# A graph attention kernel: rows that run on past a group are joined by VectorE in a shared bank instead of by ScalarE and TensorE, and two quads' logits share a bank

## The chip, the cores and the metric

The program runs on one core of one Trainium2 chip. The metric is the time of the whole program on the device in microseconds (us); of several runs the median counts. The other seven cores do nothing.

The engines of the core are TensorE (PE in the profile), VectorE (DVE), ScalarE (ACT), GpSimd (POOL) and SyncE (SP). Each has its own in-order list of instructions. They wait for each other by semaphores: an instruction that has finished adds to its engine's counter, and another engine's instruction starts when that counter has reached a value. I call such an addition a notice.

## The reference

One layer of graph attention over 12500 nodes and 200000 edges. The edges are sorted by destination `tgt`, so the edges of a node are neighbours in the list.

```python
h = relu(layernorm(x))                                  # [12500, 128]
h = (h @ W_node.T).reshape(12500, 4, 32)                # 4 heads of 32
e = (edge_attr @ W_edge.T).reshape(200000, 4, 32)
att = sum(concat([h[src], h[tgt], e], -1) * a, -1)      # [200000, 4]
att = where(att > 0, att, 0.2 * att)
m = maximum(segment_max(att, tgt), 0)
ex = exp(att - m[tgt])
deg = segment_sum(1, tgt)
denom = segment_sum(ex, tgt) + (200000 - deg) * exp(-m)
out = x + segment_sum(ex / denom[tgt] * h[src], tgt)
```

## The kernel before

The edge list is cut into 392 **groups** of 511 edges (four tiles of 128, `J`, with one place left over). Four groups are a **quad** (98 of them, `QG`). The quads are bundled into 28 **supers** of two to four quads, for which the softmax is done at once. A group's edges have at most 96 destinations, its window (`WIN`).

1. A first stage makes a table of node rows in HBM (`table`, 137 numbers a row: four heads of 32 and a one, a count, four source logits) and the target logits (`side`).
2. `fetch(q)` orders a quad's data: edge features and destinations (`fetch_edges`, L297, from SP's queue), a window of `side` and one of `x` for each group (`fetch_windows`, L484), and 16 indirect gathers of table rows by GpSimd (`gather`, L130), one for each 128 edges. The gathered rows live in a ring of eight quads (`ga_all`, L127). A gather into a place of the ring waits until TensorE has read what lay there 32 groups earlier.
3. `logits(q, i)` marks each edge's place in the window (`at`, L523) and adds up on TensorE the target's and the edge's part of the logit (L528, L531) in the bank `lg`. `add_sources` (L534) adds the three pieces up (L543) and the source's part (L545).
4. `softmax(s)` (L563) works in steps on one super: TensorE turns the logits over (`t_ps`), VectorE runs its scans for the running and final maxima, ScalarE takes exponentials, TensorE turns the results back (`ex_ps`, L632, L642). Four of its results go from TensorE to VectorE or ScalarE a step later, two within a step.
5. `sums(q)` (L702) scales a group's rows by its weights (L721), builds the one-hot matrix (`hot`, L725) and multiplies on TensorE: for each group four products into one bank `acc` of 97 rows, 96 for the window and the last one for the destination that may run on into the next group.

What matters here is that last row. A destination can go on in the next group, so the next group's sum must start from the scaled last row of the one before. Before the change this goes round four engines. The group's first edge place is empty: `complete_group` (L663) lets VectorE write the scaled row there (L668), ScalarE copies the count (L672), TensorE does the product with tile 0, which was held back (L673), and ScalarE takes the bank out (`pt`, L674), after which the next group's L668 may start:

```python
nc.vector.tensor_tensor(ga[0:1, i, 0, 0:132], before[96:97, 0:132], fc, op=mult)      # L668
nc.scalar.copy(ga[0:1, i, 0, R_CNT:R_CNT + 1], before[WIN:WIN + 1, R_CNT:R_CNT + 1])  # L672
nc.tensor.matmul(acc, hot[:, i, 0, :], ga[:, i, 0, :], start=False, stop=True)        # L673
nc.scalar.copy(pt[:, i, :], acc)                                                      # L674
```

(The first line is shortened.) `divide` (L735) then makes the quotients and adds `x`, and SP stores each group's window.

The order is written out by hand. `together` takes one step of each list in turn: in a step one group's sums are issued, one group's logits of a later quad, and in a super's first quad one part of the next softmax. The logits run five quads ahead of the sums and the gathers two quads ahead of the logits.

Of the kernel before, what the change touches and what calls it, by code (L numbers as in the profile page):

```python
# [15 lines left out]
P = 128  # L16
# [5 lines left out]
LN2 = 0.6931471805599453  # L22

# [3 lines left out]
J = 4  # L27
# [9 lines left out]
RAW, MORE = 4, 2  # L37
QUADS = 8
SETS = max(NODE_T, QG * J)
PAD = 1 << 20  # L40
# [7 lines left out]
def kernel(  # L48
# [46 lines left out]

    ident = consts.tile([P, P], F32, name="ident")
# [19 lines left out]
    cont = consts.tile([1, G], F32, name="cont")  # L116
    thru = consts.tile([1, G], F32, name="thru")
# [4 lines left out]
    raw = RAW  # L122
    assert raw == 4 < nq and MORE < quads[raw][1]
# [31 lines left out]
    with tc.manual_schedule():  # L155
# [141 lines left out]
        def fetch_edges(q):  # L297
            g0, m = quads[q]
            ea = EA[q] = load.tile([P, QG, 2, P], F32, name="ea")
            nc.sync.dma_start(ea[:, :m], edge_t[:, g0:g0 + m])  # L300
            db = DB[q] = load.tile([WIN, QG, GE], I32, name="db", bufs=2)
            nc.sync.dma_start(db[:, :m, :], dst.rearrange("(g e) -> g e", e=GE)[g0:g0 + m]
                              .unsqueeze(0).to_broadcast([WIN, m, GE]))

        with tc.tile_pool(name="node", bufs=2) as node, tc.tile_pool(
# [10 lines left out]
            def indexed():  # L316
# [27 lines left out]
                yield  # L344


                nc.vector.tensor_scalar(slot[0:1, :, 0], cont, -1.0, None, op0=OP.add)
                nc.vector.tensor_copy(is_last[0:1, :, 0], thru)
# [71 lines left out]
            for b, (t0, T) in enumerate(sets):  # L420
                load_nodes(b + 4)
                if b >= len(sets) - 3 and b - len(sets) + 3 < min(2, nq):
                    fetch_edges(b - len(sets) + 3)
# [36 lines left out]
    with tc.tile_pool(name="work", bufs=2) as work, \  # L460
# [7 lines left out]
        share_ps = const_ps[0:WIN, WIN + G:].rearrange("p (g h) -> p g h", h=H)  # L468
        nc.vector.tensor_copy(lane_ps, lane)
# [9 lines left out]
        def window(g):  # L479
            return nc.values_load(  # L480
                base[0:1, g:g + 1], engines=[mybir.EngineType.SP], min_val=0, max_val=N - 1,
                skip_runtime_bounds_check_because="a destination, which is a node")

        def fetch_windows(q):  # L484
            g0, m = quads[q]
            pw = PW[q] = load.tile([WIN, QG, SIDE], BF16, name="pw")
            xw = XW[q] = work.tile([WIN, QG, D], F32, name="xw", bufs=8)
            at = [window(g0 + i) for i in range(m)]
            for i in range(m):
                nc.sync.dma_start(pw[:, i, :], side[bass.ds(at[i], WIN), :])  # L490
            for i in range(m):
                nc.sync.dma_start(xw[:, i, :], x[bass.ds(at[i], WIN), :])  # L492

        def fetch(q):
            if q not in EA:
                fetch_edges(q)
# [11 lines left out]
        def open_logits(q):  # L508
# [5 lines left out]
            LG[q] = ps.tile([P, QG, J, PIECES, H], F32, name="lg")  # L514
# [41 lines left out]
        def run_on(n):  # L556

            unread = ps.tile([P, QG, J, PIECES, H], F32, name="lg")
            unread = unread.rearrange("p i j k h -> p (i j k h)")[:, 0:P]
            for _ in range(n):  # L560
                nc.tensor.matmul(unread, ident, ones, start=True, stop=True)

        def softmax(s):  # L563
# [15 lines left out]
            low = turned.tile([P, NE], F32, name="low")  # L579
            nc.scalar.mul(low[:R], t_ps[:R, 1:GE], SLOPE)  # L580
            yield
            att = t_ps[:R, 1:GE]
            nc.vector.tensor_tensor(att, att, low[:R], op=OP.max)
# [24 lines left out]
            if s == len(supers) - 1:  # L608
                run_on(8)
# [8 lines left out]
            ex = turned.tile([SBG * H, GE], F32, name="ex")  # L618
            nc.vector.memset(ex[:R, 0:1], 0.0)
            nc.vector.tensor_tensor(ex[:R, 1:GE], low[:R], top, op=OP.subtract)  # L620
            nc.scalar.activation(ex[:R, 1:GE], ex[:R, 1:GE], AF.Exp)  # L621

            fac = turned.tile([SBG * H, 1], F32, name="fac")
            nc.scalar.activation(fac[:R], top[:, 0:1], AF.Exp, bias=col[:R], scale=-1.0)

# [439 lines left out]
```

## Time and profile before

| | |
|---|---|
| median of three runs | 2529.13 us (2528.36 to 2543.53) |
| the profiled execution, its own time | 2525.21 us |
| its span, first to last instruction | 2523.3 us |
| PE busy | 1419.1 us (56%) |
| DVE busy | 1370.4 us (54%) |
| ACT busy | 430.2 us (17%) |
| POOL busy | 1508.5 us (60%) |
| DMA, share of the 16 engines | about 48%, 119 GB/s |
| granted TensorE clock, mean | 0.523 |

The profile is one execution. A row of the groups gives a line, the engine, the operation, the tiles, the count; then busy time, the mean time of one in ns; then the idle time of the engine before these instructions and what ended most of it. A row of the waits says which instruction waited, after the arrow who released it, and then the sum in us, the number and the longest. "Remote" stands where the profile finds no instruction beside the release. "Issue" is idle time in which it finds no wait. The share of busy time is a mean over stages: a preparation until about 300 us, a long even stage until the last gather at about 2405 us, and a tail.

### The profile page before, as it was taken

The numbers are of one execution on the slowest core, as the hardware profiler recorded it, in microseconds if no ns is written. First come the engines' busy times: TensorE is split into PE (matmuls) and PEld (weight loads), VectorE is DVE, ScalarE is ACT, GpSimd is POOL, SyncE is SP. The second block draws the span as 40 slices with busy tenths as digits, with TensorE's granted clock in tenths as the row PEclk, the third lists the DMA queues.
The fourth block names the chain that finished last, engine by engine and source line by source line (L and its number), as shares of the span: only waits on it lengthen the run. The fifth ranks groups of instructions, "written<-read, shape, count | busy, mean of one in ns | idle before, by whom it ended". The sixth has DMA issues, their size and how long they took to land. (4 is left out here: it accounts for less than half of the span.)

```text
span 2523.3 us, 29558 instructions
## 1 busy us (share of the span) xinstructions
PE 1419.1 (56%) x7317; PEld 1267.0 (50%) x7317; DVE 1370.4 (54%) x3333; ACT 430.2 (17%) x1825; POOL 1508.5 (60%) x1609
## 2 busy tenths in 40 slices
PE   4454565555655655655655555555655555546485
PEld 3444554545554544554554545554544554445375
DVE  4543465555555555555555555555555555446486
ACT  3543211111111111111111111111111111111122
POOL 6444556666666666666666666666666666666603
PEclk7665655555555555555555555555555555555556
DMA  5433465455445455445445455455445455444330
GB/s 188 145 100 97 99 148 127 115 125 128 121 122 133 114 132 129 114 122 126 120 119 129 110 123 122 116 131 127 119 119 127 112 130 128 106 104 122 86 91 17
DMA packets 214495, 299.08 MB, mean 119 GB/s; under 512 B 86121, under 2 KB 162153, under 8 KB 204914
## 3 DMA queue, kind: packets, MB, share of 16 engines
q1 hardware_dynamic: 162512, 184.97, 27.7%
q0 software_dynamic: 50112, 109.61, 19.8%
q10 hardware_dynamic: 1698, 2.58, 0.3%
q8 instruction: 61, 1.00, 0.2%
q14 instruction: 112, 0.92, 0.1%
HBM read 270.45 MB, written 26.52 MB: 118 GB/s over the span
## 5 line engine op out<-in xcount | busy, mean ns | idle before, releaser
L139 POOL DMA_INDIRECT ga<-table,srci x1494 | 1419.3, 950 | 868.4 <-issue 402.5
L730 PE MATMUL acc<-ga,hot 128*97 128x137 f32 x2352 | 648.0, 447 | 326.1 <-ACT ga L714 174.3
L730 PEld LDWEIGHTS acc<-ga,hot 128*97 128x97 f32 x2352 | 516.6, 278 | 350.6 <-ACT ga L714 180.1
L668 DVE TENSOR_TENSOR ga<-acc,facs 1x132 f32<-1x132 f32 x391 | 115.9, 297 | 627.0 <-ACT pt L674 501.5
L673 PE MATMUL acc<-ga,hot 128*97 128x137 f32 x784 | 266.9, 443 | 272.0 <-ACT ga L672 150.7
L531 PE MATMUL lg<-wblk,ea 128*128 128x8 f32 x1568 | 410.0, 359 | 0.0
L531 PEld LDWEIGHTS lg<-wblk,ea 128*128 128x128 f32 x1568 | 382.6, 310 | 0.0
L528 PEld LDWEIGHTS <-at 96*128 96x128 bf16 x1568 | 218.2, 167 | 288.6 <-DVE at L523 144.4
L674 ACT COPY pt<-acc 97x137 f32<-97x137 f32 x392 | 107.1, 273 | 1414.1 <-remote 892.0
L673 PEld LDWEIGHTS acc<-ga,hot 128*97 128x97 f32 x784 | 190.4, 279 | 303.2 <-ACT ga L672 170.6
L528 PE MATMUL lg<-pw,at 96*128 96x12 bf16 x1568 | 170.8, 182 | 227.1 <-DVE at L523 125.5
L721 DVE TENSOR_TENSOR ga<-ga,ex_ps 128x528 f32<-128x528 f32 x392 | 269.9, 689 | 35.4 <-remote 35.0
L523 DVE TENSOR_TENSOR at<-const_ps,db 96x512 bf16<-96x512 f32 x392 | 267.1, 683 | 9.4 <-DMA db<-in_dst_dram 3.6
L725 DVE TENSOR_TENSOR hot<-const_ps,slot 128x384 f32<-128x384 f32 x384 | 209.2, 545 | 0.0
L543 DVE TENSOR_REDUCE st<-lg 128x64 f32<-128x192 f32 x98 | 35.0, 357 | 153.7 <-remote 86.9
L672 ACT COPY ga<-acc 1x1 f32<-1x1 f32 x391 | 59.9, 153 | 231.5 <-DVE ga L668 109.3
L139 POOL DMA_INDIRECT ga<-in_x_dram,srci x72 | 68.5, 952 | 39.1 <-issue 21.3
L392 PE MATMUL row_ps<-wcat,hT 128*128 128x137 f32 x198 | 43.7, 377 | 56.0 <-DVE tgt L398 18.9
L632 PE MATMUL ex_ps<-ident,ex 64*128 64x64 f32 (+2 forms) x112 | 18.4, 313 | 96.3 <-ACT ex L621 70.8
L752 DVE TENSOR_TENSOR res<-pt,const_ps 96x512 f32<-96x512 f32 (+2 forms) x102 | 67.5, 662 | 4.4 <-DVE const_ps L748 0.6
L756 DVE TENSOR_TENSOR res<-res,xw 96x512 f32<-96x512 f32 (+1 forms) x99 | 66.8, 675 | 3.4
L392 PEld LDWEIGHTS row_ps<-wcat,hT 128*128 128x128 f32 x198 | 37.5, 269 | 62.0 <-ACT hn L227 16.8
(135 smaller groups left out, 1066.5 us busy)
## 6 DMA issues: line engine op xcount, KB each, us to landing
db<-in_dst_dram SPq DMA_DIRECT2D x98, 768.0 KB
ea<-in_edge_t_dram SPq DMA_DIRECT2D x98, 512.0 KB
ga<-table,srci POOLq DMA_INDIRECT x1494
xw<-in_x_dram SPq DMA_DIRECT2D x392, 48.0 KB
out_dram<-res SPq DMA_DIRECT2D x392, 48.0 KB
pw<-side SPq DMA_DIRECT2D x392, 2.2 KB
table<-row SPq DMA_DIRECT2D x9, 616.5 KB
xt<-in_x_dram SPq DMA_DIRECT2D x9, 576.0 KB
```

The costliest lines, as they stand in the source:

```text
L139: nc.gpsimd.indirect_dma_start(out=ga[:, i, j, 0:width], out_offset=None, in_=rows, in_offset=bass.IndirectOffsetOnAxis(ap=srci[:, g0 + i, ...
L392: nc.tensor.matmul(row_ps[:, t, :ROW], hT[:, t, :], wcat, start=True, stop=True)
L523: nc.vector.tensor_tensor(at[:, i, :], node_ps[0:WIN, g0 + i:g0 + i + 1].to_broadcast([WIN, GE]), db[:, i, :], op=OP.is_equal)
L528: nc.tensor.matmul(lg[:, i, j].rearrange("p k h -> p (k h)"), at[:, i, j * P:(j + 1) * P], sw, start=i + j == 0, stop=False, skip_group_ch ...
L531: nc.tensor.matmul(lg[:, i, 2 * w:2 * w + 2, 0, :], ea[:, i, w, :], wblk, start=False, stop=True, skip_group_check=True)
L668: nc.vector.tensor_tensor(ga[0:1, i, 0, 0:H * HW].rearrange("p (h w) -> p h w", w=HW), before[WIN:WIN + 1, 0:H * HW].rearrange("p (h w) -> ...
L673: nc.tensor.matmul(acc, hot[:, i, 0, :], ga[:, i, 0, :], start=False, stop=True)
L674: nc.scalar.copy(pt[:, i, :], acc)
L721: nc.vector.tensor_tensor(val, val, heads(ex)[:, :, :, g - s0].unsqueeze(3).to_broadcast([P, J, H, HW]), op=OP.mult)
L725: nc.vector.tensor_tensor(hot[:, i, :, 0:WIN], lane_ps.unsqueeze(1).to_broadcast([P, J, WIN]), slot[:, g, :].unsqueeze(2).to_broadcast([P, ...
L730: nc.tensor.matmul(acc, hot[:, i, j, :], ga[:, i, j, :], start=j == 1, stop=False)
L752: nc.vector.tensor_tensor(res[:, :n, :].rearrange("p g (h d) -> p g h d", d=HD), val[:, :, :, 0:HD], share_ps[:, :n, :].unsqueeze(3).to_br ...
```

## The change

- **Own sums.** All four products of a group are issued together, into one of three places (160 columns apart) of a bank that three consecutive groups share (`sums_place`). Nothing is put into the empty edge place. When three groups are in, `close_bank` puts on a list what is to be done from three steps on: one `carry` for each group in successive steps (VectorE multiplies the row before into `carried`, and adds it, times `thru`, to the group's last row in PSUM), and with the third `evict` (VectorE adds the three carried rows to row 0 and the counts `came` to the count column; ScalarE copies the bank to `pt`, in two parts where a quad ends within it). `divide` follows two steps after the quad's last eviction.
- The counts are worked out once in the first stage (`came`), with four small products and a scan.
- The last six quads (`ENDING`) keep the old way; before them `catch_up` empties the list.
- **Shared logits bank.** `lg` becomes one bank with two halves, one for even and one for odd quads. `add_sources` for a quad is called after the next quad's second group has been issued, instead of before its first.
- In `softmax`, the leaky slope (`low`) and the factors' copy go from ScalarE to VectorE; the factor comes out of the exponential of column 0; the exponential of minus the maximum is taken for the whole tile, so that `divide` needs no exponential; the maxima are read by the sums in PSUM instead of from a copy (`xs`). `run_on`, 18 product records in the last super whose result nobody reads, goes.
- A quad's maxima are copied into the gathered rows by one instruction instead of four, and this and the copy of `is_last` are ScalarE's in the first 14 and last 6 quads (`HELPED`) and VectorE's in between.
- `both` is a table in HBM of `x` beside `side`, made in twelve steps by SP while the first quads are fetched. From quad 14 (`APART`) a group's window is one transfer from it instead of two. From then on edge features and destinations are ordered by ScalarE's queue, after the logits two quads earlier. The four window addresses of a quad are loaded together.

The core of the diff:

```diff
+LATER = 3
+ACCS, ACC_AT = 3, 160
+HELPED = 14, 6
+ENDING = 6
+APART = 14
...
+        lg_all = ps.tile([P, 2, QG, J, PIECES, H], F32, name="lg")
...
-            LG[q] = ps.tile([P, QG, J, PIECES, H], F32, name="lg")
+            LG[q] = lg_all[:, q % 2]
...
+        def close_bank():
+            tile, used = state["bank"]
+            state["bank"] = None
+            bank = tile[0:WIN + 1, 0:ACCS * ACC_AT].rearrange("p (k r) -> p k r", r=ACC_AT)
+            bank = bank[:, 0:len(used), 0:ROW]
+            carried = work.tile([WIN + 1, ACCS, H * HW], F32, name="carried")
+            at = state["step"] + LATER
+            for k in range(len(used)):
+                todo.append((at + k, lambda k=k: carry(bank, used, carried, k)))
+            todo.append((at + len(used) - 1, lambda: evict(bank, used, carried)))
+
+        def carry(bank, used, carried, k):
...
+                nc.vector.tensor_tensor(
+                    to.rearrange("p (h w) -> p h w", w=HW),
+                    state["before"][WIN:WIN + 1, 0:H * HW].rearrange("p (h w) -> p h w", w=HW),
+                    fc[:, :, g - s0].unsqueeze(2).to_broadcast([1, H, HW]), op=OP.mult)
+                nc.vector.scalar_tensor_tensor(row, to, thru_l[:, g:g + 1], row,
+                                               op0=OP.mult, op1=OP.add)
...
+            state["before"] = bank[:, k, :]
+
+        def evict(bank, used, carried):
...
+            nc.vector.tensor_tensor(to, to, carried[WIN:WIN + 1, 0:n, :], op=OP.add)
+            nc.vector.tensor_tensor(bank[0:1, :, R_CNT], bank[0:1, :, R_CNT], came[:, g:g + n],
+                                    op=OP.add)
...
+                nc.scalar.copy(PT[q][:, i:i + len(ks), :], bank[:, ks[0]:ks[-1] + 1, :])
...
-            for i in range(m):
-                nc.scalar.copy(ga[:, i, :, R_SRC:R_SRC + H], heads(xs)[:, :, :, g0 - s0 + i])
+            copier(q)(
+                ga[:, :m, :, R_SRC:R_SRC + H],
+                heads(tops_at)[:, :, :, g0 - s0:g0 - s0 + m].rearrange("p j h g -> p g j h"))
...
-                for j in range(1, J):
-                    nc.tensor.matmul(acc, hot[:, i, j, :], ga[:, i, j, :], start=j == 1, stop=False)
-                complete()
-                begun.append((q, i, ga, hot, pt, acc, fc[:, :, g - s0]))
+                if own:
+                    acc = sums_place(q, i)
+                    for j in range(J):
+                        nc.tensor.matmul(acc, hot[:, i, j, :], ga[:, i, j, :], start=j == 0,
+                                         stop=j == J - 1, skip_group_check=True)
+                    if len(state["bank"][1]) == ACCS:
+                        close_bank()
+                    step()
...
         def all_logits(q):
-            flush()
             open_logits(q)
             for i in range(QG):
                 logits(q, i)
                 yield
+                if i == 1:
+                    flush()
+
+            if APART <= q + 2 < nq:
+                fetch_edges(q + 2, nc.scalar)
             state["logits"] = q
```

## The prediction

> **What bounds the kernel now.** The page comes first. No engine is busy for more than 60% of the span, so I look at idle time and what ends it. These are the two rows with the most idle time, and one link of the chain between the groups:
>
> ```profile
> L139 POOL DMA_INDIRECT ga<-table,srci x1494 | 1419.3, 950 | 868.4 <-issue 402.5
> ...
> L668 DVE TENSOR_TENSOR ga<-acc,facs 1x132 f32<-1x132 f32 x391 | 115.9, 297 | 627.0 <-ACT pt L674 501.5
> ...
> L674 ACT COPY pt<-acc 97x137 f32<-97x137 f32 x392 | 107.1, 273 | 1414.1 <-remote 892.0
> ```
>
> VectorE stands still for 627 us before its row copy, mostly for ScalarE's eviction, and the eviction waits for something "remote". Next the waits of GpSimd:
>
> ```profile
> POOL ga L139 <- issue: 423.8, 1384, 1.2
> POOL ga L139 <- remote: 236.6, 103, 3.5
> POOL ga L139 <- PE acc L673: 141.7, 45, 11.0
> ...
> POOL ga L139 <- PE acc L730: 19.4, 12, 2.7
> ```
>
> The 1384 waits of 0.3 us are the plain distance of two gathers, so a gather costs 0.95 + 0.30 = 1.25 us and a quad's sixteen cost 20 us. The last three rows are 160 waits of 2.49 us, **398 us** together, for TensorE's notice that a place of the ring is free. GpSimd does nothing else in the even stage: 20 us and some 4 us of waits are the quad's 24 us. So GpSimd sets the pace, and these 398 us are what can be won there. Why it waits is seen in the timeline (start, duration, instruction, idle before it):
>
> ```profile
> 1250.09 0.95 POOL L139 DMA_INDIRECT ga<-table,srci  x1 [2.58 <-remote]
> ...
> 1251.51 0.27 ACT L674 COPY pt<-acc 97x137 f32<-97x137 f32 x1 [0.86 <-PE acc L673]
> ...
> 1257.25 0.27 ACT L674 COPY pt<-acc 97x137 f32<-97x137 f32 x1 [2.18 <-PE acc L673]
> ...
> 1259.01 0.66 PE L673 MATMUL acc<-ga,hot 128*97 128x137 f32 x2
> ...
> 1264.00 0.95 POOL L139 DMA_INDIRECT ga<-table,srci  x1 [0.30 <-issue]
> ...
> 1267.29 0.27 ACT L674 COPY pt<-acc 97x137 f32<-97x137 f32 x1 [9.26 <-remote]
> ...
> 1267.53 0.94 POOL L139 DMA_INDIRECT ga<-table,srci  x1 [2.58 <-remote]
> ```
>
> The product L673 ends at 1259.67, and its eviction starts 7.6 us later, 2.3 us after GpSimd's last gather ended (1264.95) and together with GpSimd's own next start. Setting each of the 392 evictions against its product in this view, 240 follow within 0.3 us and 136 come over 1 us late. From 400 to 2200 us, of the 136 products that ended within 4.5 us of the start of a run of gathers 3 were late, of the 143 that ended 4.5 to 10.5 us after it 109. After the last gather (2405 us) none of 29 is. **So while gathers run back to back, TensorE's notices stop after about 4.5 us, and come again only about 2.3 us after GpSimd pauses.** GpSimd pauses only when it lacks such a notice itself. Then everything moves on. What of the chip causes this the trace does not show. A cycle is therefore: GpSimd fills as many groups as TensorE finished since the last pause, 5 us each, then waits 2.49 us. With 1494/4 = 373.5 groups and 160 waits TensorE gets only **2.33 groups** further in a cycle. The chain L674, L668, L672, L673 needs a new notice from TensorE for every group: two pass in the open 4.5 us, one more product is done blind, and it stands.
>
> **The change part by part** (against the profiled execution, 2525.2 us, of which 2523.3 span).
>
> *Carry by VectorE.* TensorE no longer waits for an eviction. In the changed order of instructions the carry of a bank waits for TensorE once in three groups, and then for products two steps old. This is the gain; its size is how far TensorE gets in a cycle. In the open 4.5 us one step is noticed (a step without softmax is 3.6 us of VectorE, below). From there TensorE goes on blind until VectorE needs a missing notice: a bank's comes 1 to 3 groups later with two steps of slack, a quad's logits sum 1 to 4 steps later with almost none. The earlier of the two is about 2.5 steps. In a super's softmax quad four results have one step of slack and two have none, so there it is about 2.5 in all, as now. Three quads of 3.7 and one of 2.5 make 16/(12/3.7 + 4/2.5) = 3.3 groups; I take **3.4**, since a few notices trickle through. Then 373.5/3.4 = 110 waits of 2.49 us = 274 us: **-124 us**. The ends: 2.33 stays (0), or no wait is left (-398).
>
> *What VectorE gets.* Added rows 367 times 1x132: nearest L668, 297 ns: 109 us. Eviction's 1x396 addition, 123 times: L325's 1x391 took 550 ns, L756's 96x512 675; 0.6 gives 74, and 18 for the counts at 0.15. `low`: 28 x 0.68 (L583) = 19. Copies of maxima and flags in 78 quads: 0.27 (L545) and 0.2: 36. Factors and column 0: 28 x 0.35 = 10. Sum **266 us**, 1370 to 1636. Bounds are 200 and 330. It lies beside GpSimd's 20 us a quad: VectorE then has 14.3 us a quad (7.7 for the marks and scalings L523, L721, L725, 3.3 for carries and eviction, 2.2 to divide, 0.6 for sums of logits, 0.5 for copies), and in one quad of about four 9 us of softmax (L571 to L629) as well, 23 together. Only the latter exceeds 20; of its roughly 0.9 us of new softmax work I charge half, 28 x 0.45: **+12**. Without that cover all 266 would show.
>
> Here a rule speaks against the change. The Trainium skill, *Perfetto Trace Analysis*, section "Identifying the Most-Contended Engine", takes VectorE's and GpSimd's occupancy as the bound and the busiest engine as the one to relieve. By it VectorE, at 65% the highest, is loaded further: up to +266. By the row, VectorE sits idle for 627 us before L668 alone, and GpSimd's 60% hides another 424 us of issue distance. I follow the rows: 0 outside the softmax.
>
> *Shared logits bank.* By addresses the sum L543 would come two steps after its logits, and its idle time (153.7 us of VectorE) would go. The skill's *PSUM — Partial Sum Buffer*, section "PSUM bank collisions raise a hardware error", demands that engines be kept apart by bank, not by address. The changed order does so: all 98 sums wait for the newest logits in the bank, also those of the other quad. By the addresses I would subtract up to 154 us; by the rule 0, and the wait stays. I take 0. No run here shows a collision.
>
> *ScalarE* loses L672, L714, L681 and the copies for the factors and maxima, and evicts in larger pieces: 430 us fall to some 300, off the path. It gains the edge transfers of 84 quads; one that waits for TensorE (two or more steps back) or for VectorE's newest `at` holds up eviction and exponentials behind it. Their slack is a step; 0, at worst 28 x 1 us.
>
> *SP* issues 8 transfers a quad instead of 14; nobody waits for it now (L523 for `db`: 3.6 us in all): 0. The twelve steps for `both` move some 13 MB among 299; the 24-byte pieces go while two quads lie ready: 0, at worst +10. *TensorE* has the same 3136 products for sums; 18 of `run_on` (2.8 us) go: 0, either way 3. *GpSimd* has the same gathers; four waits a group instead of one cost nothing as long as they are fulfilled, as 0.30 us stays the distance where a wait precedes. *First stage*: +3. *catch_up*: carries and eviction without sums beside, about 5 us twice, half hidden: +5; the tail has no gathers and its rows stay.
>
> Sum: 2525.2 - 124 + 12 + 5 = 2418; the added 3 lies in stages with slack. The median of the runs lies 3.9 above the profiled time: **about 2420 us**.
>
> **The rivals.**
> - *The notices hardly matter any more.* For: outside the softmax nothing but banks and logits asks TensorE, and slack in the ring is eight quads. Against: GpSimd would then never pause, and the notices come only after pauses. With 6.8 groups to a wait, 55 waits: -261, so 2280; the floor with 0 waits is 2150.
> - *Nothing is won.* The logits sum each quad and the two softmax results without slack stop VectorE, which does everything else, just as soon: 2.33 groups remain, 2525 + 17 + 4 = 2546. Also the case in which the delay of the logits sum is one in name only.
> - *Slower: VectorE becomes the bound in the softmax quads.* Now a late notice for the factors or maxima stops ScalarE; then it stops VectorE and all its marks and scalings. If TensorE gets no further per cycle and the new work of these quads (2.7 + 0.9 us) falls after the stop, 28 x 3.6 = 101: 2630. It decides as soon as VectorE's 23 us and its stops (2.3 us each) exceed the 24 us and GpSimd has no free places left. For it: 23 is close. Against: the next quads have 14 us, and the ring evens it out.
>
> **How the numbers follow.** Forecast 0.50, first rival 0.20, nothing won 0.16, slower 0.14. About 1% is what a measurement of this kernel tells from no change. Faster by more than 1% (below 2504): nearly all of the first two and a little of the third, 0.72; within 1%: 0.13; slower 0.15. The forecast's own range is 2350 to 2500. The range for 8 in 10 goes from 2230, which leaves out the ring's floor, to 2545, which takes in most of "nothing won" and leaves out the slow case.
>
> **What would show it.** Right: GpSimd's waits for TensorE number about 110 with still 2.3 to 2.6 us each; the row of idle time before L668 is gone from its successor; VectorE near 1640 us busy; gathers still 1.25 us apart; gather end near 2300 us, then the same tail of some 120 us. The logits sum should be the largest wait of VectorE. Wrong: as many waits as now, or VectorE idle for `facs` and maxima (second and third rival), or waits under 60 (first). If GpSimd's distance grows above 1.25 us, the base of the sum fails.

## The result, and the profile after

The changed kernel takes **2605.93 us** (median of four runs, 2593.63 to 2614.88); the kernel before took 2531.16 us beside it. The ratio is 1.031, 95% interval 1.0265 to 1.0353: **slower by 3%**, where 2420 us and a gain of 4% were forecast. The profiled execution took 2614.88 us, its span is 2613.1 us: 89.8 us more than the span before.

The groups of the changed kernel's profile that answer to the rows shown of before (busy time, mean ns of one, then idle time before and what ended most of it):

```profile
L155 POOL DMA_INDIRECT ga<-table,srci x1494 | 1416.6, 948 | 930.1 <-issue 338.5
...
L597 DVE TENSOR_REDUCE st<-lg 128x64 f32<-128x192 f32 x98 | 35.0, 357 | 474.6 <-remote 432.1
...
L749 ACT COPY pt<-acc 97x137 f32<-97x137 f32 (+1 forms) x184 | 65.4, 389 | 1510.3 <-DVE acc L742 546.5
L731 DVE SCALAR_TENSOR_TENSOR acc<-carried,thru,acc 1x132 f32<-1x132 f32 x367 | 138.9, 379 | 83.5 <-PE acc L845 36.5
L727 DVE TENSOR_TENSOR carried<-acc,facs 1x132 f32<-1x132 f32 x367 | 110.2, 300 | 12.6 <-ACT pt L749 1.3
```

The 627 us of idle time before the carried row are gone: L727 waits 12.6 us. But the sum of a quad's logits, L597, now waits 474.6 us, 432.1 of it for a late notice ("remote"). Its row before the change was

```profile
L543 DVE TENSOR_REDUCE st<-lg 128x64 f32<-128x192 f32 x98 | 35.0, 357 | 153.7 <-remote 86.9 <-issue 31.4 <-PE acc L673 29.1
```

GpSimd's waits now (sum, number, longest):

```profile
POOL ga L155 <- issue: 358.6, 1148, 1.9
POOL ga L155 <- PE acc L845: 324.4, 204, 14.4
POOL ga L155 <- remote: 154.5, 106, 3.6
...
POOL ga L155 <- PE lg L585: 45.3, 67, 2.5
```

Before, the waits for TensorE were 160 with 398 us. Now the last three of these rows are 377 waits with 524 us: more of them, and more time. One stretch of the timeline shows what they look like (start, duration, instruction, idle time before it):

```profile
1105.84 0.94 POOL L155 DMA_INDIRECT ga<-table,srci  x1 [0.30 <-issue]
1105.88 2.14 PE L845 MATMUL acc<-ga,hot 128*97 128x137 f32 x8
...
1110.30 0.52 PE L845 MATMUL acc<-ga,hot 128*97 128x137 f32 x1 [0.35 <-issue]
1110.83 0.94 POOL L155 DMA_INDIRECT ga<-table,srci  x1 [0.30 <-issue]
1111.70 0.39 PE L845 MATMUL acc<-ga,hot 128*97 128x137 f32 x1 [0.88 <-issue]
1112.08 0.94 POOL L155 DMA_INDIRECT ga<-table,srci  x1 [0.30 <-issue]
1113.11 0.61 PE L845 MATMUL acc<-ga,hot 128*97 128x137 f32 x2 [1.02 <-issue]
1113.38 0.94 POOL L155 DMA_INDIRECT ga<-table,srci  x1 [0.36 <-PE acc L845]
...
1117.74 0.36 DVE L597 TENSOR_REDUCE st<-lg 128x64 f32<-128x192 f32 x1 [6.19 <-remote]
1117.75 0.94 POOL L155 DMA_INDIRECT ga<-table,srci  x1 [2.00 <-remote]
```

A group's four products (eight records) took 2.14 us at 1105.88. The next group's eight records come singly or in twos, from 1108.85 to 1115.17, about one or two to each gather, with idle time between them that nothing in the profile explains. VectorE stands at L597 for 6.19 us and starts together with GpSimd's next gather, as ScalarE's eviction did before the change. So TensorE itself stalls in mid-group now; before the change no matmul of the sums or logits from 1050 to 2250 us stood for over 0.25 us behind one of its own line; now 63 records do.

**Where the 89.8 us arise.** I set the first scaling of each quad (L721 before, L835 after) of the two profiles side by side. At quad 12 the changed kernel is 16.8 us behind, at quad 18 19.3, at quad 36 53.6, at quad 90 73.9, at the end 89.8. The loss has four places: 17 us in the first quads, 34 between quads 18 and 36, 20 over the long even stage, 16 from quad 90 on. Of these 16, 14 lie between the middle of quad 91 and the start of quad 92, where `catch_up` empties the list.

**Pauses.** I also took each gather's idle time beyond the plain 0.30 us, after 330 us, and called it a pause from 1.5 us up:

| kernel | pauses | their sum, us | mean | short ones | sum |
|---|---|---|---|---|---|
| before | 133 | 302 | 2.27 | 17 | 17 |
| after | 109 | 316 | 2.90 | 95 | 73 |
| c1_check_apart | 110 | 274 | 2.49 | 99 | 73 |
| c4_sum_first | 111 | 268 | 2.42 | 84 | 60 |
| c3_both | 103 | 251 | 2.44 | 91 | 69 |
| d2_all_three | 117 | 320 | 2.73 | 20 | 16 |
| e1_no_carry | 113 | 268 | 2.37 | 23 | 17 |
| k1_before_pairs | 121 | 262 | 2.17 | 30 | 34 |

Together 319 us before and 389 after. That is 70 us, and the last gather starts 61 us later (2457 instead of 2396, which the text ahead gave as about 2405). The rows of c1 and c4, two runs explained below, add up to 347 and 328 us: the edit of c1 takes 42 of the 70 us away, and that of c4 another 19.

### The profile page after: what moved, and what is told of

The parts are those of the page before. It is cut to its first block, busy times and chain, and to the rows that moved or that the text cites. A ratio compares the mean times of both kernels' runs of the same rounds, so it can differ in the third digit from the quotient of the medians.

```text
span 2613.1 us, 27591 instructions
## 1 busy us (share of the span) xinstructions
PE 1436.7 (55%) x7303; PEld 1259.7 (48%) x7303; DVE 1653.2 (63%) x4169; ACT 240.9 (9%) x638; POOL 1505.5 (58%) x1609
## 5 line engine op out<-in xcount | busy, mean ns | idle before, releaser
L845 PE MATMUL acc<-ga,hot 128*97 128x137 f32 x2944 | 790.7, 444 | 218.7 <-DVE hot L839 111.6
L845 PEld LDWEIGHTS acc<-ga,hot 128*97 128x97 f32 x2944 | 651.4, 278 | 257.9 <-issue 170.9
L582 PEld LDWEIGHTS <-at 96*128 96x128 bf16 x1568 | 202.7, 161 | 539.2 <-DVE at L577 252.6
L582 PE MATMUL lg<-xw,at 96*128 96x12 bf16 x1568 | 171.2, 180 | 442.5 <-DVE at L577 224.0
L597 DVE TENSOR_REDUCE st<-lg 128x64 f32<-128x192 f32 x98 | 35.0, 357 | 474.6 <-remote 432.1
L835 DVE TENSOR_TENSOR ga<-ga,ex_ps 128x528 f32<-128x528 f32 x392 | 270.1, 689 | 34.4 <-ACT ga L826 28.1
L749 ACT COPY pt<-acc 97x137 f32<-97x137 f32 (+1 forms) x184 | 65.4, 389 | 1510.3 <-DVE acc L742 546.5
L731 DVE SCALAR_TENSOR_TENSOR acc<-carried,thru,acc 1x132 f32<-1x132 f32 x367 | 138.9, 379 | 83.5 <-PE acc L845 36.5
L727 DVE TENSOR_TENSOR carried<-acc,facs 1x132 f32<-1x132 f32 x367 | 110.2, 300 | 12.6 <-ACT pt L749 1.3
L625 PE MATMUL t_ps<-ident,U 128*64 128x128 f32 (+2 forms) x112 | 29.5, 418 | 148.9 <-DVE U L599 129.3
L807 POOL TENSOR_SCALAR hot<-lane,slot 128x96 f32<-128x96 f32 x32 | 17.0, 549 | 98.5 <-issue 92.8
L741 DVE TENSOR_TENSOR acc<-acc,carried 1x396 f32<-1x396 f32 x124 | 69.7, 562 | 4.3
```

The costliest lines, as they stand in the source:

```text
L582: nc.tensor.matmul(lg[:, i, j].rearrange("p k h -> p (k h)"), at[:, i, j * P:(j + 1) * P], sw, start=i + j == 0, stop=False, skip_group_ch ...
L727: nc.vector.tensor_tensor(to.rearrange("p (h w) -> p h w", w=HW), state["before"][WIN:WIN + 1, 0:H * HW].rearrange("p (h w) -> p h w", w=H ...
L731: nc.vector.scalar_tensor_tensor(row, to, thru_l[:, g:g + 1], row, op0=OP.mult, op1=OP.add)
L741: nc.vector.tensor_tensor(to, to, carried[WIN:WIN + 1, 0:n, :], op=OP.add)
L835: nc.vector.tensor_tensor(val, val, heads(ex)[:, :, :, g - s0].unsqueeze(3).to_broadcast([P, J, H, HW]), op=OP.mult)
L845: nc.tensor.matmul(acc, hot[:, i, j, :], ga[:, i, j, :], start=j == 0, stop=j == J - 1, skip_group_check=True)
```

## The experiments

Ratios are to the kernel before, in runs on the same chip. The kernel before took 2521 to 2531 us on these chips, except with d1, d2, n0 and n1, where it took 2550; a ratio of that group is not compared with another's to within 1%. Where I give a lag, it is that of a profiled execution behind the profile of before, read as above.

### Two orders inside the change: c1 to c4

The guard `checked()` compares 128 rows of destinations four times. Before the change a step of other work lay between the transfer and the comparison; the change had moved them into one step, on SP's queue. The diff shown with the change leaves this part out. c1 puts a quad between them (one of the four steps that it adds to the guard is shown):

```diff
                 nc.sync.dma_start(rows[:n], dst_rows[g0:g0 + n, 0:NE + 1])
+                yield
                 falls = turned.tile([P, NE], F32, name="low")
```

> The changed kernel with one edit in checked(): between the order of the 128 rows of destinations and their comparison (L931, L933) VectorE gets a whole quad of other work, so that it does not stand at L933 for the transfer. Theory A (the four waits of 54.0 us in all hold up everything, since between quads 24 and 36 the changed kernel falls behind by some 45 us): the wait of L933 is gone, the lag at quad 36 is below 15 us, about 2560 us. Rival B (VectorE has slack there, the ring of gathers covers the stops): within 10 us of 2606.

VectorE's waits from 700 to 980 us in the changed kernel:

```profile
DVE low L933 <- DMA ex<-in_dst_rows_dram: 54.0, 4, 14.1
DVE st L597 <- remote: 31.5, 4, 9.6
```

These four waits are all of the guard's in the kernel. In c1 they are gone, and the lag at quad 36 is 22.6 us instead of 53.6. Measured: **2587.63 us, 1.0265** (1.0226 to 1.0304). Theory A holds for the place, at less than its price: 31 us at quad 36 in the profile, 11 to 21 us in the ratios (after to c1, where the intervals still overlap, and c2 to c3, where they do not).

c2 gives the sum of logits two steps of slack, from quad 8 on (the first eight quads keep their order in a branch that is not shown):

```diff
-            for i in range(QG):
-                logits(q, i)
-                yield
-                if i == 1:
-                    flush()
+            for i in range(0, QG, 2):
+                logits(q, i)
+                logits(q, i + 1)
+                yield
...
+            yield
+            add_sources(q)
+            yield
```

> The changed kernel with the logits of a quad issued two groups a step in its first two steps, and their sum (L597) in the fourth, from quad 8 on: the newest logits in the shared bank are then two steps old for every sum. Theory A (VectorE's wait of 432 us at L597 for TensorE's late notice took the place of the wait at L668 and hides the gain of the carry): the wait at L597 falls below 200 us and the time by 40 to 120 us, to 2490 to 2565. Rival B (GpSimd's own waits set the pace, wherever VectorE stands): L597's wait moves to other VectorE rows, and the time stays within 15 us of 2606.

Measured: **2574.79 us, 1.0213** (1.0186 to 1.0240). VectorE's waits in c2:

```profile
DVE low L629 <- remote: 168.5, 18, 20.0
DVE st L597 <- PE acc L845: 104.9, 42, 8.5
DVE st L597 <- remote: 91.1, 12, 10.8
DVE acc L731 <- remote: 67.4, 12, 12.5
```

L597's idle time falls to 203 us (196 in these two rows), where theory A asked for less than 200; but the softmax's first step (L629) and the carry (L731) now stand for late notices themselves. About 25 us (a ratio lower by 0.0096) are won, below theory A's range. Both theories hold in part: the wait moves, and a little is won.

c3 has both edits.

> Both edits, of c1 and c2. If both theories A hold: 45 us less than c2, 2445 to 2520, faster than the kernel before. If only the first holds: about 2560. If neither: about 2606.

Measured: **2555.02 us, 1.0129** (1.0103 to 1.0154): the two gains roughly add up, but the result stays above the 2520 that was expected at most, and slower than before.

c4 is c1 with `flush()` again ahead of the next quad's first group:

```diff
+            flush()
             open_logits(q)
...
-                if i == 1:
-                    flush()
```

> c1, and in addition the sum of a quad's logits put back ahead of the next quad's first group (as before the change), with the bank still shared. In the changed kernel 28 of the 98 sums come within the softmax's first step and wait for logits issued in the same step (192 us of 477 us), the others one step later. Theory A (the missing slack of these 28 costs): L597's idle time falls by 100 us or more and the time is 15 to 40 us below c1. Rival B (the notice comes only when GpSimd pauses, and a step more or less does not matter): within 10 us of c1.

Measured: **2560.64 us, 1.0155** (1.0126 to 1.0183), 0.011 or some 28 us below c1, as in theory A. By moving the sum behind the second group, the change had put 28 of the 98 sums into the softmax's first step. There the newest logits in the shared bank had been issued in the same step: 192.5 us of idle time before these 28, 6.9 us each, against some 48 us before the change. But c4 moves all 98 sums. From c1 to c4 L597's idle time falls from 477 to 382 us, just short of the 100 us that theory A asked for: 40 of these 96 us at the 28 sums, 55 at the other 70. So the 28 us are not the price of the 28 sums alone. In c4 the lag is 18.4 us at quad 24 and still 19.8 at quad 90: with the guard and the sum put right the even stage is level with the kernel before from there on, and the 31.5 us by which c4's profile is longer arise before quad 24 and after quad 90.

### The order of the products: d1 and d2

```diff
-                    for j in range(J):
+                    for j in reversed(range(J)):
```

This is d1, made on the changed kernel; d2 is the same on c3.

> The changed kernel with the four products of a group issued from tile 3 to tile 0 instead of 0 to 3. A gather into tile 0 then waits for the last product, and the next three need no wait for TensorE (one wait a group as before the change, 360 in all instead of 1438). Theory A (the finer waits hurt: GpSimd goes on gather by gather behind TensorE, with 64 short waits of 0.79 us from 1050 to 2250 us where before there were 9): the short waits go, and 20 to 60 us with them, 2540 to 2585. Rival B (the pace is set by how far TensorE and VectorE get between two pauses, and the same idle time of GpSimd comes in longer pieces): within 12 us of 2606.

> c3_both with the reversed order of products of d1 in addition. If theory A of d1 holds: 20 to 60 us below c3's 2555, so about 2515, level with the kernel before or faster. If B holds: within 12 us of 2555.

d1: **2606.92 us, 1.0226** (1.0197 to 1.0255). d2: **2562.49 us, 1.0048** (1.0034 to 1.0061). The short waits go as expected: from 1050 to 2250 us, 14 in d1 instead of 64. But the pauses grow: all idle time of GpSimd beyond 0.30 us is 360 us in d1 (389 in the changed kernel) and 335 in d2 (320 in c3). By the ratios 20 us are won in both, by absolute medians nothing, as the kernel before was slower on that chip; which of the two is right is not known. The finer waits are not settled as a cost; the idle time mostly goes into longer pieces, as rival B has it.

### Without the gathers, and with gathers that never wait: n0, n1, g1

```diff
-            for j in range(n):
-                nc.gpsimd.indirect_dma_start(
-                    out=ga[:, i, j, 0:width], out_offset=None, in_=rows,
-                    in_offset=bass.IndirectOffsetOnAxis(ap=srci[:, g0 + i, j:j + 1], axis=0))
+            nc.sync.dma_start(ga[:, i, 0:n, 0:width],
+                              rows[0:n * P, 0:width].rearrange("(j p) r -> p j r", p=P))
```

n0 is made on the kernel before, n1 on the changed one. Both leave the choice of rows out, so their outputs are not the layer's; only their times count.

> The kernel before, with each group's four indirect gathers of GpSimd replaced by one plain transfer of 512 fixed rows of the table from SP's queue (same bytes, other rows, so the sources are not the reference's). Theory A (while GpSimd gathers back to back, TensorE's notices come late, and this sets the pace): evictions follow their products within 0.5 us in the even stage, VectorE's idle time before L668 falls below 150 us, time 1900 to 2200. Rival C (something other delays the notices, TensorE itself or ScalarE): the late evictions stay, and the time is within 5% of 2529.

> The changed kernel with the same replacement. Theory A: VectorE's wait at L597 falls from 477 to below 60 us, and VectorE, with 1650 us of work, is then over 85% busy in the even stage and sets the pace: 1850 to 2100, and not faster than n0 by much, as it has 280 us more of VectorE's work. Rival C: L597 keeps its wait, over 2450.

n0: **1967.72 us**; n1: **1994.47 us**. Theory A holds in both. In n0 all 392 evictions follow their product within 0.04 us, and the carry's row waits 123.6 us instead of 627.0. In n1 the largest waits of VectorE are

```profile
DVE low L931 <- DMA ex<-in_dst_rows_dram: 66.7, 4, 21.3
DVE st L595 <- PE lg L583: 38.2, 31, 4.6
```

(lines two lower than in the changed kernel): the sum of logits waits 38.2 us instead of some 475, and the guard's four waits head the list. VectorE is busy for 182.0 of 200 us from 1050 to 1250 us, where n0's is for 139.0. So with the same bytes but without GpSimd's gathers both kernels lose over 550 us. The changed one is then bound by VectorE: from quad 36 to 88 it is 91% busy. There n1 is not slower but faster, 17.2 us a quad against n0's 18.3; the 27 us are lost in the first eight quads, between quads 20 and 26, where the guard is, and at quad 92. Nor do the two price the carry. n0 has a limit of its own, as SP's queue now carries the rows too: VectorE waits 316.3 us there for earlier stores of results.

```profile
DVE res L750 <- DMA out_dram<-res: 316.3, 62, 8.1
```

g1 lets the gathers run without any wait for TensorE:

```diff
-        ga = GA[q] = ga_all[:, q % QUADS]
+        ga = ga_all[:, q % 4]
+        GA[q] = ga if q < 5 else ga_all[:, 4 + q % 4]
```

> The changed kernel with gathers that never wait for TensorE from quad 5 on: they write into four places of the ring that nobody reads, and the sums read four other places that hold zeros (so the output leaves the gathered rows out). Same gathers, same products. Theory A (TensorE's notices come only while GpSimd pauses): the gathers run 1.25 us apart to their end near 2150 us, and sums advance slowly until then and fast after it, or steadily with notices 7 to 10 us late. Rival D (1.48 us a gather): the distance of two gathers grows to about 1.48 us though nothing waits for TensorE, and they end near 2400 us.

Measured: **3803.06 us, 1.51**. Two stretches (busy us of PE, PEld, DVE, ACT, POOL, each with its number of instructions, then clock, DMA share, GB/s), and VectorE's largest wait:

```profile
500.00:2300.00 1800.00, 149.02 (x642) 119.05 (x641) 144.93 (x333) 12.56 (x38) 1382.74 (x1289) 0.50 0.23 59
2300.00:3700.00 1400.00, 1014.21 (x5207) 902.89 (x5208) 1227.44 (x2969) 90.24 (x220) 0.00 (x0) 0.51 0.35 95
```

```profile
DVE st L600 <- remote: 1068.7, 14, 147.8
```

For 1800 us, while gathers come without a pause, VectorE works for 145 us and about two groups are summed in 100 us; once the gathers have ended, it is 22 groups in 100 us. DMA engines are 23% busy, so their bandwidth as a whole is not what is short. And TensorE's own instructions come singly, one to every one or two gathers:

```profile
1402.44 0.17 PE L585 MATMUL lg<-xw,at 96*128 96x12 bf16 x1 [3.12 <-issue]
1403.43 1.10 POOL L158 DMA_INDIRECT ga<-table,srci  x1 [0.30 <-issue]
1403.84 0.10 PEld L585 LDWEIGHTS <-at 96*128 96x128 bf16 x1 [2.70 <-issue]
1404.83 1.10 POOL L158 DMA_INDIRECT ga<-table,srci  x1 [0.30 <-issue]
1405.23 0.17 PE L585 MATMUL lg<-xw,at 96*128 96x12 bf16 x1 [2.62 <-issue]
```

Theory A holds for the sums: slow until the gathers end, fast after it. Rival D is right in one thing: after some 170 gathers without a pause their distance grows from 1.25 to 1.40 us, and the last one starts at 2289 us, between the two theories' ends. So a quad's sixteen gathers cost 22.4 us when nothing ever stops them. If that distance is the floor, the even stage of the kernel before, at 23.8, had only some 1.4 us a quad to give; that is an estimate, for why the distance grows, and whether it would with a few short pauses, no run here shows.

### One release a quad: f0, f1, f2

```diff
-    ga_all = consts.tile([P, QUADS, QG, J, ROW], F32, name="ga")
+    ga_pool = ctx.enter_context(tc.tile_pool(name="ga_pool", bufs=QUADS))
```

f1 is made on c4, f2 on c3, f0 on the kernel before.

> c4 (comparison a quad later, sum first), and the ring of gathered rows made of eight tiles, one for each quad, instead of one block: the first gather of a quad then waits for TensorE to have finished the whole quad eight before, and no other gather waits for it; so only products that somebody else waits for give a notice (1528 notices of TensorE in the program instead of 2286 or more, 90 waits of GpSimd for TensorE instead of 1438). Theory A (TensorE's notices queue up while GpSimd gathers, and stop it and VectorE; fewer notices and fewer stops of GpSimd are faster): at most 100 pauses of some 2.5 us, GpSimd's waits for TensorE below 300 us, 2400 to 2510. Rival D (a gather needs 1.48 us of some shared path, of which 0.23 us show only as pauses; no order of the consumers changes that): a quad keeps its 23.8 us, within 12 us of c4's 1.0155 of before.

> The same ring on c3 (sums of logits two steps late) instead of c4: 1641 notices. Theory A: as f1, within 15 us of it. Rival D: within 12 us of c3's 1.0129 of before.

> The kernel before with the ring of eight tiles alone (2271 notices instead of 2383; 90 waits instead of 359). There every group's carry needs a new notice of TensorE. Theory A: GpSimd pauses at most once a quad, but the chain gets only some 2.6 groups further between two pauses, so the pauses become longer: within 40 us of 2529, either way. Rival D: within 12 us.

f1: **2561.56 us, 1.0145** (1.009 to 1.020). f2: **2670.21 us, 1.059** (1.0528 to 1.0652). f0: **2842.99 us, 1.127** (1.1206 to 1.1333). GpSimd's waits in f0:

```profile
POOL ga L146 <- PE acc L680: 689.4, 83, 32.1
```

Fewer pauses do not help: there are 85 in f1 and f2 and 88 in f0, but their means are 3.94, 5.22 and 7.14 us. A pause lasts until TensorE has got through the whole quad. Theory A's price is wrong in all three. Rival D's time came true in f1 alone; f0's quad takes 27.3 us, not 23.8. Nor do fewer notices end the stalls in mid-group: f1's trace has 1507 notices of TensorE where c4's has 2324, but 118 such stalls from 1050 to 2250 us where c4 has 60. These stalls do not order the kernels either: c3 has 203 and e1 64, and both are faster than the changed kernel with its 63. The Trainium skill, *TensorE: Matmul & The Clock Gate*, section "The cost: per-tile semaphore tail", fits 26.3 ns to each semaphore increment at the end of small matmuls packed into one array; carried over to these products, 817 notices fewer would be an estimate of 21 us. c4 and f1 are equal within their intervals, but f1's pauses changed too, so no run here shows that gain or refutes it. Why f2 is so much worse than f1 stays open.

### What is left: the carry, the tail and the first quads

```diff
-ENDING = 6
+ENDING = 84
```

e1 is d2 with the old carry from quad 14 on.

> d2 with the old carry (VectorE writes the row, product of tile 0 last, eviction by ScalarE) from quad 14 on instead of only in the last six. Theory A (the carry by VectorE buys longer runs between two pauses, but in the even stage GpSimd's gathers leave only some 1.4 us a quad to win, and the tail pays for VectorE's added work): the even stage keeps 23.7 to 24.0 us a quad, the tail after the last gather is 10 to 25 us shorter, 0.990 to 1.000 of before. Rival E (the carry by VectorE does speed up the even stage of d2, and other parts of the change eat it): the even stage slows to over 24.5 us a quad, ratio above 1.015.

Measured: **2496.85 us, 0.9899** (0.9853 to 0.9945), the lowest median of all, below d2's by 66 us, or by 0.015 (some 38 us) in the ratios. From 1050 to 2250 us a quad takes 23.2 us instead of d2's 23.9, and GpSimd's waits in that stretch are

```profile
POOL ga L155 <- issue: 235.8, 742, 1.1
POOL ga L155 <- remote: 99.2, 40, 4.2
POOL ga L155 <- PE lg L585: 37.8, 15, 3.8
POOL ga L155 <- PE acc L788: 26.7, 14, 3.0
```

The tail after the last gather is 131.5 us against d2's 149.7. Theory A holds in sign and in the tail, and the even stage is better than it said: here the carry by VectorE does not merely win nothing, it loses. How much is less sure. h3 and i1 (below) differ in little but the carry too, on chips where the kernel before took 2527.7 and 2527.6 us; there it costs 8.5 us (2524.16 against 2515.66). With it, d2's VectorE has 15.8 us of work a quad, without it 13.3; the pauses are as many (117 and 113) but 2.73 us long instead of 2.37.

h1 keeps the old carry for ten quads at the end, and gives the leaky slope back to ScalarE:

```diff
-HELPED = 14, 6
-ENDING = 6
+HELPED = 14, 10
+ENDING = 10
...
-            nc.vector.tensor_scalar(low[:R], att, SLOPE, None, op0=OP.mult)
+            nc.scalar.mul(low[:R], att, SLOPE)
```

> d2 with the old carry for the last ten quads instead of six, so that the list is emptied while gathers still run, ScalarE's copies for these ten, and the leaky slope on ScalarE as before. Theory A (the tail is bound by VectorE: 119.6 us busy of 156 against 97.0 of 127 before): the stretch after the last gather falls from 150 to about 130 us and the ratio from 1.0048 to 0.994 to 1.000. Rival F (the tail is bound by the chain of TensorE and ScalarE): 1.002 or more.

h2 leaves the joined table out and orders all edges from SP:

```diff
-            if q < APART and q not in EA:
+            if q not in EA:
                 fetch_edges(q, nc.sync)
-            next(join_steps, None)
...
-            if APART <= q + 2 < nq:
-                fetch_edges(q + 2, nc.scalar)
```

> d2 without the joined table and with all edge transfers from SP's queue, as before the change. Theory A (the first 12 quads fall behind by some 13 us while the joined table is made, as its DMA share is 0.89 there from 300 to 400 us against 0.58; nobody waits for SP later): the lag at quad 12 falls below 6 us, ratio 0.998 to 1.002. Rival G (the joined windows and ScalarE's edge transfers help the even stage): no gain or a loss, 1.005 to 1.02.

h3 is both.

> d2 with the edits of h1 and h2 together. If both theories A hold: 0.988 to 0.996 of before, faster than both kernels; if neither, 1.005.

h1: **2543.08 us, 1.0077** (1.0050 to 1.0104). h2: **2540.63 us, 1.0053** (1.0025 to 1.0080). h3: **2524.16 us, 0.9986** (0.9964 to 1.0008). d2's ratio comes from the other chip, so I compare medians: 19, 22 and 38 us below d2's 2562.49; against d2's ratio (1.0048) h1 and h2 show nothing. Neither ratio comes as low as its theory A; both lie where rivals F and G put them. The profiles speak for both mechanisms of theory A all the same. The stretch after the last gather, first of the changed kernel, then of h1:

```profile
2457.03:2613.10 156.07, 89.44 (x481) 78.85 (x480) 119.54 (x301) 19.89 (x78) 20.51 (x36) 0.58 0.20 51
```

```profile
2402.30:2534.70 132.40, 85.83 (x450) 76.74 (x450) 98.77 (x245) 21.54 (x89) 20.69 (x36) 0.58 0.20 49
```

VectorE is busy for 119.5 us of the one and for 98.8 of the other (97.1 before), and the stretch is 24 us shorter; d2's was 149.7. In h2 the lag of 9.6 us at quad 12 becomes a lead of 2.7, and the DMA share from 300 to 400 us is 0.62 instead of 0.85. ScalarE orders its first edges at 450 us, when quad 8 begins; there d2's lag of 7.7 us is a lead of 3.8 in h2 already. So what d2 loses in the first eight quads is the joined table's.

k1 is c2's edit on the kernel before; i1 is e1 with h2's edit and the slope on ScalarE.

> The kernel before with one edit: a quad's logits two groups a step in its first two steps and their sum in the fourth, from quad 8 on, as in c2. If the earlier logits are what made e1_no_carry 1% faster than before: 0.985 to 0.997 of before, the even stage 23.2 to 23.6 us a quad. If the other parts of the change did it (copies, factors and maxima, one release a group): 0.998 to 1.005.

> e1_no_carry (old carry from quad 14 on, logits early, comparison apart, products from tile 3 to 0) with h2's edit (no joined table) and the leaky slope on ScalarE as before. Both together took 0.6% from d2 in h3_all, part of that by the shorter list in the tail, which e1 has already. If they add to e1: 0.982 to 0.989 of before, the fastest of all. If the joined windows and ScalarE's edge transfers help e1: 0.990 to 0.998.

k1: **2512.78 us, 0.9928** (0.9903 to 0.9953). i1: **2515.66 us, 0.9937** (0.9914 to 0.9961). The early logits alone make the kernel before 0.7% faster. h2's edit and the slope do not add to e1; the second expectation of i1 holds. The intervals of e1, k1 and i1 overlap: all three beat the kernel before by 0.6 to 1.0%, and which is best is not settled.

## Why the prediction was wrong

- **What bounds the kernel.** The picture was right and is now shown: without gathers both kernels run below 2000 us (n0, n1), and with gathers that never pause almost nothing moves (g1).
- **Carry by VectorE, the step that failed.** The forecast's term was -124 us: TensorE would get 3.4 groups further between two waits instead of 2.33, so 110 waits instead of 160, each of 2.49 us as before. By the rows it was counted in there are 377 waits with 524 us. By the pauses there are 109, but this near hit is partly luck: by that measure there were 133 before, so half of the expected fall. And the two other parts failed. The mean pause did not stay: 2.27 us became 2.90. And 95 short waits of 0.77 us came on top where there had been 17, which I had not counted. In all 389 us of idle time instead of 319: the term -124 became about +70. (It was also too large by itself, as 0.30 us of each wait are in the base of 20 us already: -110.)
- **What the +70 consist of.** 42 us go when the guard's comparison is moved apart (c1), 19 more when the sum of logits goes back (c4). Then 111 pauses of 2.42 us and 84 short waits stand against 133 of 2.27 and 17: 328 us, level with the kernel before. So the carry by VectorE itself won nothing in the even stage; with the old carry in its place the kernel is faster (e1 against d2, i1 against h3). Why TensorE gets no further is not shown. That VectorE's larger load does it is argued: those pairs differ in the carry and so in both load and order, and no run separates the two. But f0 to f2 show plainly that fewer pauses can each be longer, and in c3, c4, d2, f1, h1, h2, h3 and i1 GpSimd's idle time stays at 312 to 335 us with anything from 85 to 127 pauses, where the kernel before has 319 with 133.
- **The base of 20 us.** Gathers stay at 1.25 us in the changed kernel, as forecast. But that is not a floor that holds: without pauses it is 1.40 us (g1). If that is the floor, the whole even stage had some 1.4 us a quad to give, an estimate of 120 us for 88 quads. The forecast claimed nearly all of it, and the first rival (2280) much more.
- **Four waits a group cost nothing.** Not settled (d1, d2): the short waits came from them, but without them the pauses grew.
- **VectorE's added work.** Forecast 1636 us busy, measured 1653.2. The added row (L731) takes 379 ns, not 297: 138.9 us for my 109. The rule of the busiest engine, which stood against the change in the prediction, came true only without the gathers, where VectorE is 91% busy (n1). The charge of 12 us for the softmax quads looked at VectorE's work there and not at what it would wait for: moving the sums out of the softmax's first step and a step earlier elsewhere gave 28 us (c4 against c1).
- **Shared logits bank, "the wait stays".** Counting on the bank and not on the addresses was right: the wait did not go. But "stays" was wrong: 153.7 us became 474.6. I had read that all 98 wait for the newest logits, and not looked at how old these are in the softmax quads.
- **ScalarE's edge transfers and the joined table.** 0 was taken, with at worst 28 for ScalarE and 10 for the table; the first quads lose 17 us. h2 undoes both and takes d2's lag of 9.6 us there away; up to quad 8, where ScalarE's transfers only begin, that is the table's.
- **Left out altogether:** the guard's comparison in one step with its transfer, 54 us of VectorE's waits, 11 to 31 us of time. It was in the diff, in a part that I took for bookkeeping.
- **Tail, "its rows stay", and 5 us for `catch_up`.** In the tail there are no gathers to hide VectorE: 97.1 us of its work became 119.5, and the stretch grew from 127.4 to 156.1 us. Where `catch_up` empties the list the lag grows by 14 us, not 5. In h1 this happens at quad 88, with gathers still running; the lag grows by 13 us there too, but is down to what it was within a quad.
- **The rivals.** The second, "nothing is won", named what the runs show of the carry: the sum of logits stops VectorE just as soon. The sum as VectorE's largest wait stands among the signs of being right, and came; it fits this rival as well. The third (2630, VectorE the bound in the softmax quads) gave the nearest number, mostly by luck. A little of it is there: VectorE's waits for `facs` (20.6 us) and the copied maxima (11.8 us) are small, but before the scan of the group ends' maxima (L646) it stands for 53.1 us, against 9.3 before the change. For the most part VectorE stopped at L597 instead, in the softmax's first step (6.9 us a time) and outside it (4.0).

## What to carry to other kernels

Where one engine's stalls are the price of another's notices, count not only how often it will wait but how much work must still be done when the notice comes: that work is the length of the wait. A transfer and its first use in one step are a stop of the whole engine, also in code that is only a guard; read every moved line of a diff for that. Extra work on an engine with slack in the average stage shows in the stage where nothing hides it, here the tail: 22 us more work made it 29 us longer.

## What the runs showed of the hardware

- While GpSimd issued indirect gathers without a pause, TensorE all but stood: two groups in 100 us instead of 22, at a DMA share of 0.23 (g1). Its instructions then came one to a gather or two. With plain transfers in place of the gathers all 392 evictions followed their products within 0.04 us (n0). Whether notices, instructions or something else are held up, the runs do not tell.
- The distance of two indirect gathers was 1.25 us in a run of some 170, and mostly 1.40 us after that (g1).
- In runs at six different times, on several chips, the same kernel before took 2521 to 2531 us five times and 2550 once: a ratio from one chip did not carry to another to within 1%.
